# A group's closing spread over four passes, and the redo of a tied row block prepared beside the last block's products

## The chip, the cores and the metric

The kernel runs on one core of a Trainium2 chip. The metric is the device time of one execution in microseconds; times are medians of several executions. The spans, passes and waits below come from one profiled execution of each kernel.

## The reference, cut to what matters

Two graph layers work on x of 4096 rows and 256 columns. Layer 0 is an attention with four heads, masked by a 4096 x 4096 adjacency matrix; its output is normalized per row and added to x. Layer 1 makes two steps of an attention that keeps, in each row, the largest probabilities up to a sum of 0.9.

```python
e = where(adj > 0, leaky_relu(src + dst), NEG_INF)            # layer 0, four heads
out = softmax(e) @ h                                           # per head
x = x + layernorm(out) * gamma + beta                          # "closing" in the kernel
...
for n in range(2):                                             # layer 1
    A = top_p(softmax(Xa W.. ), 0.9)                           # ties: in order of index
    Xf = R @ Xf ; Xa = A @ Xa
    Z = Z + Xf @ U1[n].T + Xa @ U2[n].T
x = x + layernorm(h + Z)
```

Rows in which values tie exactly at the threshold must keep them in order of index. The kernel computes all 32 row blocks as if there were no ties, and repeats a block where there are some ("redo"). With these inputs one block of step 1 is repeated and none of step 0.

## The kernel before

Layer 0 goes over four groups of 8 row blocks. Each group has four passes (heads), each pass 16 steps `p`: VectorE makes two masks, TensorE does 32 products. What a pass leaves is evacuated in the next; after the fourth head the group is closed, in twelve small pieces ("closers": four of statistics, eight row blocks).

```python
ax = l0a.tile([P, 4, G0 * P], BF16, name="ax")                 # adjacency tile, 1 MB, by GpSimd's queue
nc.gpsimd.dma_start(ax, adj_t[...])
...
def close(i):
    xb = l0s.tile([P, D], F32, name="xb")                      # pool l0s: two buffers
    nc.sync.dma_start(xb, x[ts(b, P), :])
    ob = l0s.tile([P, D], F32, name="ob")
    nc.scalar.activation(ob, o[:, i, :], AF.Identity, scale=..., bias=...)
    nc.vector.tensor_mul(ob, ob, gamma_r)
    nc.gpsimd.tensor_tensor(xb, xb, beta_r, ALU.add)
    nc.vector.tensor_add(xb, xb, ob)
    nc.sync.dma_start(x1_d[b], xb)
    ...
# in mask_stage (SyncE and GpSimd issue the transfers)
    if h == 1 and p % 2:
        nc.sync.dma_start(adj_d[...], ax[p // 2])              # 1 MB: a copy for later
    if h == H - 1 and ig + 1 < NB // G0 and p % 2:
        next_ax.append(edges(ig + 1, p // 2))                  # next group's tiles: fourth pass
# main loop, one closer per step
    if p != PAIRS - 1 and p > 1 and later:
        later.pop(0)()                                         # three evacuations, then twelve closers
```

At the end, step 1 chooses the kept values of block 31, multiplies, contributes, and then `repaired` counts the ties and calls `again` for each tied block: logits, exponentials, a branch around a repeated search, the ranking of ties on VectorE (`untied`), and then products and contribution.

## Time and profile before

| | before |
|---|---|
| time | 3289.59 us (3287.62 to 3290.06, 3 runs) |
| span of the profiled execution | 3283.7 us |
| TensorE, VectorE, ScalarE, GpSimd busy | 90%, 81%, 59%, 38% |
| layer 0, first to last product | 801.8 us |
| the same rows as the prediction's four passes: sum | 205.1 us |

No engine is idle for long in sum, so what counts is where TensorE stops. The prediction shows the two places. The other view that matters, as it turned out, is this one: what SyncE waited for before it could issue its transfers, in the first pass after a group (337.3 to 399.8 us), where six of the eight row blocks were closed. The columns are the wait, its sum in us, how often, and the longest. In all lines PE is TensorE (PEld its weight loads), DVE VectorE, ACT ScalarE, POOL GpSimd; SPq, ACTq and POOLq are the instruction queues of SyncE, ScalarE and GpSimd.

```profile
SPq L341 <- DMA x_d<-xb: 12.1, 6, 3.5
```

Line 341 loads x rows into `xb`; before it can, the store out of the same buffer must have landed. Six such waits of at most 3.5 us did little harm: VectorE stood 0.6 us in all for the rows in that pass. The transfers' medians in that pass (KB each, us from issue to landing) were short:

```profile
x_d<-xb SPq DMA_DIRECT2D x6, 128.0 KB, 2.3
xb<-in_x_dram SPq DMA_DIRECT2D x6, 128.0 KB, 2.0
```

The share of 0.63 in the prediction's row of this pass is an average: up to 368.0 us it is 0.99, and from 374.7 us on, when the row blocks were closed, 0.36.

### The profile page before, as it was taken

The numbers are of one execution on the slowest core, as the hardware profiler recorded it, in microseconds if no ns is written. First come the engines' busy times: TensorE is split into PE (matmuls) and PEld (weight loads), VectorE is DVE, ScalarE is ACT, GpSimd is POOL, SyncE is SP. The second block draws the span as 40 slices with busy tenths as digits, with TensorE's granted clock in tenths as the row PEclk, the third lists the DMA queues.
The fourth block names the chain that finished last, engine by engine and source line by source line (L and its number), as shares of the span: only waits on it lengthen the run. The fifth ranks groups of instructions, "written<-read, shape, count | busy, mean of one in ns | idle before, by whom it ended". The sixth has DMA issues, their size and how long they took to land. (4 is left out here: it accounts for less than half of the span.)

```text
span 3283.7 us, 51700 instructions
## 1 busy us (share of the span) xinstructions
PE 2967.7 (90%) x19213; PEld 2416.0 (74%) x19213; DVE 2651.4 (81%) x5002; ACT 1950.6 (59%) x2903; POOL 1253.2 (38%) x1793
## 2 busy tenths in 40 slices
PE   4499899898989999986899999999879999999994
PEld 2399799797977888873677777777747777777783
DVE  6599899898976555555999999999479988888864
ACT  5588687786862110027577777674376777776721
POOL 3200100101000000004889889887044656656520
PEclk8699999999999999997899999999979999999997
DMA  9726639366225455420000000000200000000000
GB/s 258 229 83 154 193 115 255 115 156 191 73 93 182 163 178 164 164 76 1 13 15 17 18 15 19 17 15 20 68 2 15 25 20 25 22 22 25 20 20 12
DMA packets 198307, 268.41 MB, mean 82 GB/s; under 512 B 13728, under 2 KB 155552, under 8 KB 198048
## 3 DMA queue, kind: packets, MB, share of 16 engines
q1 hardware_dynamic: 152272, 207.99, 19.0%
q0 software_dynamic: 16896, 33.56, 5.7%
q10 hardware_dynamic: 28880, 23.48, 2.3%
q8 instruction: 153, 2.51, 0.3%
q14 instruction: 106, 0.87, 0.1%
HBM read 226.77 MB, written 71.76 MB: 91 GB/s over the span
## 5 line engine op out<-in xcount | busy, mean ns | idle before, releaser
L800 PE MATMUL acc<-X,eT 128*128 128x256 f32 x4160 | 976.2, 380 | 0.6 <-ACT eT L794 0.5
L800 PEld LDWEIGHTS acc<-X,eT 128*128 128x128 f32 x4160 | 761.8, 191 | 89.5 <-ACT eT L794 1.6
L291 PE MATMUL acc<-ut,m 128*128 128x195 bf16 (+1 forms) x8192 | 732.2, 249 | 84.0 <-DVE m L279 47.4
L291 PEld LDWEIGHTS <-m 128*128 128x128 bf16 x8192 | 704.9, 98 | 111.1 <-DVE m L279 64.8
L272 ACT ACTIVATE g<-sr,d_big 128x1024 bf16<-128x1024 f32 x512 | 550.8, 1178 | 50.7 <-DVE m L278 41.0
L618 ACT ACTIVATE void<-e,c 128x2048 int8<-128x2048 f32 x244 | 490.5, 2010 | 0.6
L432 PE MATMUL racc<-hl,ar 128*128 128x512 f32 x2048 | 470.0, 391 | 16.2 <-issue 11.1
L611 ACT ACTIVATE e<-mm,nm 128x1024 f32<-128x1024 f32 x256 | 286.2, 1118 | 332.4 <-PE mm L488 329.2
L432 PEld LDWEIGHTS racc<-hl,ar 128*128 128x128 f32 x2048 | 385.7, 189 | 100.2 <-issue 11.9
L792 PEld LDWEIGHTS tp<-ident,e 128*128 128x128 f32 x2080 | 246.5, 142 | 229.5 <-issue 142.5
L794 ACT COPY eT<-tp 128x512 f32<-128x512 f32 x520 | 304.0, 585 | 182.0 <-PE tp L792 182.0
L792 PE MATMUL tp<-ident,e 128*128 128x128 f32 x2080 | 326.6, 281 | 64.8 <-DVE e L728 35.3
L278 DVE TENSOR_TENSOR m<-g,ax 128x2048 bf16<-128x2048 bf16 x256 | 311.8, 1218 | 43.4 <-ACT g L272 39.6
L707 DVE MAX8 cand<-big 128x8 f32<-128x228 f32 (+1 forms) x1088 | 343.9, 394 | 0.1
L279 DVE TENSOR_TENSOR m<-ax,m 128x2048 bf16<-128x2048 bf16 x256 | 316.6, 1237 | 26.9 <-DVE m L278 1.4
L488 PE MATMUL mm<-kT,qT 64*128 64x512 f32 x1024 | 304.5, 678 | 33.6 <-ACT e L611 33.6
L428 DVE CAST ar<-at 128x1024 fp32r<-128x1024 bf16 x256 | 177.6, 694 | 174.0 <-PE racc L432 170.3
L694 DVE SCALAR_TENSOR_TENSOR big<-e,lowered 128x4096 f32<-128x4096 f32 x64 | 286.8, 4481 | 20.9 <-POOL lowered L639 20.9
L728 DVE SCALAR_TENSOR_TENSOR e<-e,found 128x4096 f32<-128x4096 f32 x64 | 288.2, 4503 | 0.0
L443 ACT ACTIVATE xf<-xf,rinv 128x256 f32<-128x256 f32 x64 | 32.7, 510 | 373.3 <-DVE xf L442 371.0
L648 POOL TENSOR_TENSOR sums<-sums 128x4 f32<-128x4 f32 (+1 forms) x64 | 106.3, 1661 | 353.4 <-ACT void L618 231.3
L488 PEld LDWEIGHTS mm<-kT,qT 64*128 64x128 f32 x1024 | 84.0, 195 | 130.3 <-issue 66.8
(241 smaller groups left out, 3245.8 us busy)
## 6 DMA issues: line engine op xcount, KB each, us to landing
at<-adj_d SPq DMA_DIRECT2D x256, 256.0 KB, 2.8
ut<-uv_d SPq DMA_DIRECT2D x60, 784.0 KB, 4.3
ax<-in_adj_t_dram POOLq DMA_DIRECT2D x32, 1024.0 KB, 13.1
adj_d<-ax SPq DMA_DIRECT2D x32, 1024.0 KB, 11.7
uv_d<-parts ACTq DMA_DIRECT2D x32, 392.0 KB, 7.4
xf<-xf_d SPq DMA_DIRECT2D x65, 128.0 KB, 2.0
sr<-s_d SPq DMA_DIRECT2D x16, 512.0 KB, 4.7
xf_d<-xf ACTq DMA_DIRECT2D x64, 128.0 KB, 2.2
```

The lines of the kernel that those rows point to most:

```text
L272: nc.scalar.activation(g[:, c, :], shared[k].sr, AF.Relu, scale=BIG, bias=d_big[:, h, j:j + 1])
L278: nc.vector.tensor_tensor(m[0], g, a, ALU.min)
L279: nc.vector.tensor_tensor(m[1], a, m[0], ALU.subtract)
L291: nc.tensor.matmul(shared[k].acc[i][:, t, :cols], m[t][:, c, ts(i, P)], shared[k].ut[j // QUARTER][:, j % QUARTER, t, :cols], start=(j == ...
L432: nc.tensor.matmul(acc[i].rearrange("p s d -> p (s d)"), ar[:, c, ts(i, P)], hl[hop][:, j].rearrange("p s d -> p (s d)"), start=(j == 0), ...
L488: nc.tensor.matmul(pm[:, h, :], q[ts(h, DA), :], kT[ts(h, DA), ts(c, 512)], start=True, stop=True)
L618: nc.scalar.activation(void, r.e[:, ts(h, N // 2)], (AF.Relu, AF.Sign)[i], bias=r.c1, scale=-1.0, accum_out=r.sums[:, h, 2 + i:3 + i])
L707: nc.vector.max(cand[:, s, :], big[:, edges[s]:edges[s + 1]])
L728: nc.vector.scalar_tensor_tensor(r.e, r.e, r.t, r.e, ALU.is_ge, ALU.mult, accum_out=kept)
L792: nc.tensor.transpose(pt[:, i, :], r.e[:, ts(4 * g + i, P)], ident)
L794: nc.scalar.copy(eT, pt)
L800: nc.tensor.matmul(r.acc[:, 0, :], eT[:, i, :], cur[:, j, :], start=(j == 0), stop=(j == NB - 1))
```

## The change

The intent is twofold. In layer 0 the closers are no longer done one per step in the first pass (and the start of the second), but one every third step over all four passes, so that VectorE's small surplus over TensorE can pay for them. At the end, the counting of ties and the preparation of the redo up to the ranking move in front of the products of block 31, so that VectorE ranks while TensorE multiplies.

```diff
             later = []
+            closers = []
...
-                return [both, three, divided] + (closing(ig) if h == H - 1 else [])
+                if h == H - 1:
+                    closers.extend(closing(ig))
+                return [both, three, divided]
...
-                    if p != PAIRS - 1 and p > 1 and later:
-                        later.pop(0)()
+                    if p != PAIRS - 1 and p > 1:
+                        if later:
+                            later.pop(0)()
+                        elif closers and p % 3 == 0:
+                            closers.pop(0)()
...
-    def again(n, b, kT, qT, nm, t, cur, failed):            # all of the redo, after the last block
+    def prepared(R):      # copies of q, logits, exponentials, [If failed: search], ranking
+    def completed(R, cur):  # loads, transposes, products, contribution
...
+            def beginning():
+                finish(blocks[NB - 2])
+                with tc.If(number(R, R.undone) > 0):
+                    prepared(R)
...
-                attend(r, cur, blocks.get(b - 1), blocks.get(b + AHEAD))
+                attend(blocks[b], cur, blocks.get(b - 1), blocks.get(b + AHEAD),
+                       {5: last_chosen, 6: looked} if b == NB - 2 else {})
...
+            attend(r, cur, blocks[NB - 2], None, {0: beginning})
```

(The pools `l0u` and `o` change their number of buffers too.)

More of the change, by code (lines that the diff above doesn't have):

```diff
@@ L152, in gat_then_top_p_diffusion @@
     with tc.tile_pool(name="l0", bufs=1) as l0, tc.tile_pool(name="l0a", bufs=9) as l0a, \
-            tc.tile_pool(name="l0u", bufs=6) as l0u:
+            tc.tile_pool(name="l0u", bufs=5) as l0u:
         sd_c = l0.tile([P, 2, H, NB], F32, name="sd_c")
@@ L251, in gat_then_top_p_diffusion @@
             out_rows = {}
-            later = []
+            later, closers = [], []
             def sources(k):
@@ L298, in evacuate @@
                 if h == 0:
-                    out_rows[ig] = l0o.tile([P, G0, D], F32, name="o")
+                    out_rows[ig] = l0o.tile([P, G0, D], F32, name="o", bufs=2)
                     for i in range(G0):
@@ L395, in gat_then_top_p_diffusion @@
                     products(k, p, ms.pop(n))
-                    if p != PAIRS - 1 and p > 1 and later:
-                        later.pop(0)()
+                    if p != PAIRS - 1 and p > 1:
[3 more added lines that the diff above has]
+                            closers.pop(0)()
                 later.extend(evacuate(k))
-                while later:
-                    later.pop(0)()
+                for last in later + closers:
+                    last()
     xp = ctx.enter_context(tc.tile_pool(name="xp", bufs=1))
@@ L578, in col, with totals @@
         return small.tile([P, 1], F32, name=name, bufs=bufs or 4)
-    def totals(t):
+    def totals(t, name):
         pn = ps2.tile([P, 4, P], F32, name="tp")[:, 0, :]
         nc.tensor.matmul(pn[:1, :NB], ones[:, :1], t, start=True, stop=True)
-        n = small.tile([1, 1], F32, name="n", bufs=1)
+        n = small.tile([1, 1], F32, name=f"n_{name}", bufs=1)
         nc.vector.reduce_sum(n, pn[:1, :NB], axis=AX.X)
-        n_i = small.tile([1, 1], I32, name="n_i", bufs=1)
+        n_i = small.tile([1, 1], I32, name=f"n_i_{name}", bufs=1)
         nc.vector.tensor_copy(n_i, n)
-        ns_i = small.tile([1, NB], I32, name="ns_i", bufs=1)
+        ns_i = small.tile([1, NB], I32, name=f"ns_i_{name}", bufs=1)
         nc.vector.tensor_copy(ns_i, pn[:1, :NB])
@@ L773, in untied @@
         nc.vector.scalar_tensor_tensor(r.e, ties, r.t, r.e, ALU.mult, ALU.add, accum_out=kept)
-        r.scale = col("scale")
         nc.vector.reciprocal(r.scale, kept)
@@ L820, in contributed, with attend @@
             nc.tensor.matmul(r.acc[:, 1, :], zT[:, i, :], u_s[2 * r.n + i // KC][:, i % KC, :], start=(i == 0), stop=(i == 3))
-    def attend(r, cur, before, ahead):
+    def attend(r, cur, before, ahead, between={}):
         if ahead:
@@ L844, in attend, with questioned @@
                 first_probe(ahead, PROBED.index(g))
+            if g in between:
+                between[g]()
         scaled(r)
-    def again(n, b, kT, qT, nm, t, cur, failed):
-        sp, dve, act = b
-        r = SimpleNamespace(n=n, b=sp)
-        q = rows.tile([2 * DA, P], F32, name="a_q", bufs=1)
-        shift = col("a_nm", 1)
-        nc.scalar.copy(q, qT[:, ds(act * P, P)])
-        nc.scalar.copy(shift, nm[:, ds(act, 1)])
-        r.e = l1e.tile([P, N + NB], F32, name="e1")[:, :N]
-        sums = small.tile([P, 2, 4], F32, name="sums", bufs=6)
-        ev = r.e.rearrange("p (h c n) -> p h c n", h=2, c=4)
-        loads(r)
-        z, r.t = col("a_z", 1), col("a_t", 1)
-        def exponentials_again():
-            for c in range(4):
-                nc.scalar.activation(ev[:, :, c, :], logits(q, kT, c), AF.Exp, bias=shift, accum_out=sums[:, c // 2, c % 2:c % 2 + 1])
-            nc.vector.tensor_tensor(sums[:, 0, :2], sums[:, 0, :2], sums[:, 1, :2], ALU.add)
-            nc.vector.tensor_tensor(z, sums[:, 0, 0:1], sums[:, 0, 1:2], ALU.add)
-        exponentials_again()
-        nc.vector.tensor_copy(r.t, t[:, ds(dve, 1)])
-        if n + 1 < STEPS:
-            r.x = rows.tile([P, D], F32, name="a_x", bufs=1)
-            nc.vector.tensor_copy(r.x, X[:, ds(dve, 1), :].rearrange("p o d -> p (o d)"))
-        with tc.If(failed > 0):
-            m = small.tile([P, N // 1024], F32, name="m4", bufs=1)
-            for c in range(N // 1024):
-                nc.vector.tensor_reduce(m[:, c:c + 1], logits(q, kT, c), AX.XY, ALU.max)
-            nc.vector.tensor_reduce(shift, m, AX.X, ALU.max, negate=True)
-            exponentials_again()
-            searched(r.e, z, r.t, junk)
-        untied(r, z, junk)
-        eT = [turn(r, 0)]
-        for g in range(NB // 4):
-            if g + 1 < NB // 4:
-                eT.append(turn(r, g + 1))
-            gather(r, eT[g], g, cur)
-        scaled(r)
-        contributed(r, contribute(r))
-        finish(r)
-        finish_scale(r)
-        finish_rows(r)
-    def repaired(n, kT, qT, nm, far, cur, found):
+    everyone = [ET.PE, ET.DVE, ET.Activation, ET.Pool, ET.SP]
+    def questioned(far, found):
         t, after, eighth = found
@@ L906, in repaired @@
         nc.vector.tensor_tensor(undone, undone, failed, ALU.add)
-        engines = dict(engines=[ET.PE, ET.DVE, ET.Activation, ET.Pool, ET.SP], min_val=0, max_val=6 * P * NB)
-        with tc.If(nc.values_load(totals(undone)[1], **engines) > 0):
-            numbers = totals(failed)[1]
-            failed_n = nc.values_load(numbers, **engines)
-            counts = totals(undone)[0]
-            which, key, ids = (small.tile([1, NB], F32, name=f"a_{x}", bufs=1) for x in ("which", "key", "ids"))
-            nc.vector.tensor_scalar(which, counts, 0, None, ALU.is_gt)
-            blocks_n = small.tile([1, 1], F32, name="a_n", bufs=1)
-            blocks_i = small.tile([1, 1], I32, name="a_ni", bufs=1)
-            nc.vector.reduce_sum(blocks_n, which, axis=AX.X)
-            nc.vector.tensor_copy(blocks_i, blocks_n)
-            nc.vector.tensor_tensor_scan(key, ones[:1, :NB], zero[:1].to_broadcast([1, NB]), 0.0, ALU.add, ALU.add)
-            nc.vector.tensor_tensor(key, key, which, ALU.mult)
-            for i in range(NB // 8):
-                nc.vector.max(ids[:, ts(i, 8)], key)
-                nc.vector.match_replace(key, ids[:, ts(i, 8)], key, -1.0)
-            ids_i, rest = (small.tile([1, NB], I32, name=f"a_{x}", bufs=1) for x in ("ids_i", "rest"))
-            nc.vector.tensor_scalar(ids_i, ids, -1.0, 0.0, ALU.add, ALU.max)
-            with tc.For_i(0, nc.values_load(blocks_i, engines=engines["engines"], min_val=0, max_val=NB), 1):
-                b = [nc.values_load(ids_i[:, :1], engines=[x], min_val=0, max_val=NB - 1) for x in (ET.SP, ET.DVE, ET.Activation)]
-                again(n, b, kT, qT, nm, t, cur, failed_n)
-                nc.vector.tensor_copy(rest[:, 1:], ids_i[:, 1:])
-                nc.vector.tensor_copy(ids_i[:, :NB - 1], rest[:, 1:])
@@ new lines, in questioned, with counted, number @@
+        return failed, undone
+    def counted(R):
+        R.undone, R.failed = totals(R.undone, "u"), totals(R.failed, "f")
+        R.e = l1e.tile([P, N + NB], F32, name="e1")[:, :N]
+        R.z, R.t, R.scale = (col(f"a_{x}", 1) for x in ("z", "t", "scale"))
+        R.rest_i = small.tile([1, 1], I32, name="a_rest_i", bufs=1)
+        R.ids_i = small.tile([1, NB], I32, name="a_ids_i", bufs=1)
+    def number(R, total):
+        return nc.values_load(total[1], engines=everyone, min_val=0, max_val=6 * P * NB)
@@ new lines, in chosen @@
+    def chosen(R):
+        which, key, ids = (small.tile([1, NB], F32, name=f"a_{x}", bufs=1) for x in ("which", "key", "ids"))
+        nc.vector.tensor_scalar(which, R.undone[0], 0, None, ALU.is_gt)
+        blocks_n = small.tile([1, 1], F32, name="a_n", bufs=1)
+        nc.vector.tensor_tensor_scan(key, ones[:1, :NB], zero[:1].to_broadcast([1, NB]), 0.0, ALU.add, ALU.add)
+        nc.vector.tensor_tensor(key, key, which, ALU.mult)
+        for i in range(NB // 8):
+            nc.vector.max(ids[:, ts(i, 8)], key)
+            nc.vector.match_replace(key, ids[:, ts(i, 8)], key, -1.0)
+        nc.vector.tensor_scalar(R.ids_i, ids, -1.0, 0.0, ALU.add, ALU.max)
+        nc.vector.reduce_sum(blocks_n, which, axis=AX.X)
+        nc.vector.tensor_scalar(R.rest_i, blocks_n, -1.0, None, ALU.add)
@@ new lines, in index, with exponentials_again @@
+    def index(R, engine):
+        return nc.values_load(R.ids_i[:, :1], engines=[engine], min_val=0, max_val=NB - 1)
+    def prepared(R):
+        act, dve = index(R, ET.Activation), index(R, ET.DVE)
+        q = rows.tile([2 * DA, P], F32, name="a_q", bufs=1)
+        shift = col("a_nm", 1)
+        nc.scalar.copy(q, R.qT[:, ds(act * P, P)])
+        nc.scalar.copy(shift, R.nm[:, ds(act, 1)])
+        nc.vector.tensor_copy(R.t, R.table[:, ds(dve, 1)])
+        sums = small.tile([P, 2, 4], F32, name="sums", bufs=6)
+        ev = R.e.rearrange("p (h c n) -> p h c n", h=2, c=4)
+        def exponentials_again():
+            for c in range(4):
+                nc.scalar.activation(ev[:, :, c, :], logits(q, R.kT, c), AF.Exp, bias=shift, accum_out=sums[:, c // 2, c % 2:c % 2 + 1])
+            nc.vector.tensor_tensor(sums[:, 0, :2], sums[:, 0, :2], sums[:, 1, :2], ALU.add)
+            nc.vector.tensor_tensor(R.z, sums[:, 0, 0:1], sums[:, 0, 1:2], ALU.add)
+        exponentials_again()
+        with tc.If(number(R, R.failed) > 0):
+            m = small.tile([P, N // 1024], F32, name="m4", bufs=1)
+            for c in range(N // 1024):
+                nc.vector.tensor_reduce(m[:, c:c + 1], logits(q, R.kT, c), AX.XY, ALU.max)
+            nc.vector.tensor_reduce(shift, m, AX.X, ALU.max, negate=True)
+            exponentials_again()
+            searched(R.e, R.z, R.t, junk)
+        untied(R, R.z, junk)
@@ new lines, in completed @@
+    def completed(R, cur):
+        r = SimpleNamespace(n=R.n, b=index(R, ET.SP), e=R.e, scale=R.scale)
+        dve = index(R, ET.DVE)
+        loads(r)
+        if r.n + 1 < STEPS:
+            r.x = rows.tile([P, D], F32, name="a_x", bufs=1)
+            nc.vector.tensor_copy(r.x, X[:, ds(dve, 1), :].rearrange("p o d -> p (o d)"))
+        eT = [turn(r, 0)]
+        for g in range(NB // 4):
+            if g + 1 < NB // 4:
+                eT.append(turn(r, g + 1))
+            gather(r, eT[g], g, cur)
+        scaled(r)
+        contributed(r, contribute(r))
+        finish(r)
+        finish_scale(r)
+        finish_rows(r)
+        rest = small.tile([1, NB], I32, name="a_rest", bufs=1)
+        nc.vector.tensor_copy(rest[:, 1:], R.ids_i[:, 1:])
+        nc.vector.tensor_copy(R.ids_i[:, :NB - 1], rest[:, 1:])
@@ L932, in finish, with repaired @@
+    def repaired(R, cur):
+        with tc.If(number(R, R.undone) > 0):
+            completed(R, cur)
+            with tc.For_i(0, nc.values_load(R.rest_i, engines=everyone, min_val=0, max_val=NB), 1):
+                prepared(R)
+                completed(R, cur)
     def finish(r):
@@ L999, in gat_then_top_p_diffusion, with chosen_kept @@
                 probed(3)
-            for b in range(NB):
+            def chosen_kept(b):
                 r = blocks[b]
@@ L1022, in gat_then_top_p_diffusion, with last_chosen, looked @@
                     masked(r)
+            R = SimpleNamespace(n=n, kT=kT, qT=qT, nm=nm, table=found[0])
+            def last_chosen():
+                chosen_kept(NB - 1)
+                R.failed, R.undone = questioned(far, found)
+            def looked():
+                counted(R)
+                chosen(R)
+            def beginning():
+                finish(blocks[NB - 2])
+                with tc.If(number(R, R.undone) > 0):
+                    prepared(R)
+            for b in range(NB - 1):
+                chosen_kept(b)
                 if b + AHEAD < NB:
                     blocks[b + AHEAD] = began(n, b + AHEAD, kT, qT, nm, sg, thr, c1)
-                attend(r, cur, blocks.get(b - 1), blocks.get(b + AHEAD))
+                attend(blocks[b], cur, blocks.get(b - 1), blocks.get(b + AHEAD),
+                       {5: last_chosen, 6: looked} if b == NB - 2 else {})
             r = blocks[NB - 1]
-            finish(blocks[NB - 2])
+            attend(r, cur, blocks[NB - 2], None, {0: beginning})
             contributed(r, contribute(r))
@@ L1033, in gat_then_top_p_diffusion @@
                 finish_rows(blocks[b])
-        repaired(n, kT, qT, nm, far, cur, found)
+        repaired(R, cur)
 _INS = ['x', 'adj', 'adj_t', 'w', 'a', 'gamma', 'beta', 'w1_t', 'w2_t', 'w3_t', 'u1_t', 'u2_t', 'ln_g', 'ln_b']
```

## The prediction

> **What bounds the kernel now.** I read the page first (busy shares and slices), then the chain of waits that ended last, then the timeline of two places that the change touches, and last the busy time of single stretches. The page says that TensorE is busy 90% of 3283.7 us, VectorE 81%, so no engine has enough idle time for a large win; a gain has to come from places where TensorE waits. Two such places are changed.
>
> The first is the end. The chain that ended last, in order of time (start us, us, what; cut in the middle and at the end):
>
> ```profile
> 3226.52 2.35 DVE junk L758
> ...
> 3233.40 4.33 DVE rank L768
> ...
> 3240.41 4.50 DVE rank L768
> ...
> 3247.32 4.50 DVE e L773 x2
> 3251.82 0.14 issue
> 3251.96 1.94 PE tp L792 x8
> 3253.90 3.54 PE acc L800 x8
> ```
>
> This is the redo of the one row block with tied values in step 1 (64 blocks should give 4096 product matmuls counted as on the page, it shows 4160: one block more). The timeline of that stretch shows what TensorE does meanwhile (start, us, engine, line, operation, idle before and its releaser):
>
> ```profile
> 3203.95 0.18 DVE L585 TENSOR_REDUCE n<-tp 1x1 f32<-1x32 f32 x1 [15.66 <-PE tp L583]
> ...
> 3217.50 6.50 PE L488 MATMUL mm<-kT,a_q 64*128 64x512 f32 x16 [10.03 <-ACT a_q L853]
> ...
> 3251.96 1.94 PE L792 MATMUL tp<-ident,e 128*128 128x128 f32 x8 [27.96 <-DVE e L773]
> ```
>
> TensorE stands still for 10.03 us, works 6.5 us on logits, and stands still for another 27.96 us while VectorE ranks the ties; just before that VectorE itself was idle 15.66 us, in the last block's products. The two idle times don't overlap, and nothing but program order keeps them apart.
>
> The second place is layer 0. I cut its 16 passes (4 groups of rows by 4 heads, 512 matmuls each) at the first product of each. Busy time in the four passes of the second group (window, length, then PE, PEld, DVE, ACT, POOL, granted clock, DMA share, GB/s):
>
> ```profile
> 337.30:399.80 62.50, 48.97 (x515) 45.19 (x513) 53.76 (x85) 40.34 (x51) 10.83 (x11) 0.95 0.63 200
> 399.80:450.20 50.40, 46.39 (x512) 44.56 (x512) 46.73 (x49) 41.73 (x55) 6.61 (x6) 0.97 0.45 128
> 450.20:496.30 46.10, 44.45 (x515) 43.42 (x513) 42.19 (x38) 39.35 (x50) 0.00 (x0) 1.00 0.25 82
> 496.30:542.40 46.10, 44.44 (x515) 43.42 (x514) 41.86 (x38) 39.37 (x50) 5.18 (x7) 1.00 1.04 250
> ```
>
> The first two passes carry the closing of the group before. A pass without it takes 46.1 us (46.6 us where it evacuates the first head), so the closing costs 16.4 + 3.8 = 20.2 us, three times: 60.6 us. The closing of the fourth group comes after the last product and stays there.
>
> **What the Trainium skill says.** (1) "TensorE: Matmul & The Clock Gate", What's actually happening: the array falls to half clock after an idle window of some 3.4 us. The trace agrees: the eight transposes at 3251.96 took 1.94 us against 1.07 us for eight in mid-block, and the first eight products 3.54 us against 1.73 us a group later. (2) "SBUF — State Buffer", Who interferes with whom: a GpSimd operation and a VectorE operation in a two-port mode block each other. The trace fits: some mask subtractions take 1.57 us instead of 1.23 us in the passes where GpSimd adds beta, none in the others. (3) "Runtime: NRT & Kernel Launch", Instruction fetch mechanics: a taken branch to a far target stalls the fetch. The trace agrees: at the end of step 0, where nothing is redone, VectorE's jump over the redo took 3.1 us from its compare (2340.70) to its next instruction (2343.83), TensorE's 1.05 us.
>
> **Part 1, layer 0.** The same 12 closers are kept per group, one after every third step at p = 6, 9, 12 of four passes (p = 3 goes to the evacuation), as the order of instructions confirms. From the timeline: a mask pair on VectorE comes every 2.46 us, TensorE takes 2.72 us per step, so VectorE gains 0.26 us a step. The evacuation's three adds use up the lead until p = 6. A pair of statistics costs VectorE 1.08 us (356.13 to 357.21), a closed row block 1.53 us (377.78 to 379.32). With zero lead at p = 6, the lead regained before a closer bites is 0.5 us for the first and 0.75 us for the second and third, 2.0 us per pass; the rest is stall.
> - Pass of three statistics: 3 x 1.08 - 2.0 = 1.2 us.
> - One statistics, two closes: 1.08 + 3.06 - 2.0 = 2.1 us. This pass also starts with VectorE's row sums of the first head, which ScalarE's evacuation awaits. VectorE now comes there 1.7 us later than after a free pass (evacuation 2.0 us before the pass turns; now about 0.3). I add 1.7 us; today's pass, late in the same way, begins with a step of 4.74 instead of 3.54 us.
> - Two passes of three closes: 2 x (4.6 - 2.0) = 5.2 us.
> - Eight additions on GpSimd that now mostly hit a mask operation: 6 x 0.34 = 2 us.
>
> Together 12.2 us per group against 20.2: 8 us x 3 = 24 us. Today's dear items, two steps of 7.0 and 6.4 us where the first closed block waits for GpSimd's power (2.68 us) and then ScalarE, vanish, because 8 us pass between last statistics and first close; I take 26 us. The buffer for weights going from 6 to 5 costs nothing: a quarter is loaded two ahead and at most four are live.
>
> **Part 2, the end.** Now the last block's choice is made in the products of block 30, the counts there too (two small matmul groups, 0.3 us on TensorE), and logits, exponentials and tie ranking of the redo come after the first group of products of block 31. Working forward from the old times: group 0 of block 31 ended at 3188.7, +0.3 is 3189.0; indices are on hand at about 3185.2 (counts 3181.4, 1.2 us of reads, 2.6 us of choosing as from 3213.87 to 3216.39) and ScalarE's copy of q at about 3188.6, so the logits start at 3189.3. TensorE is warm there: instead of 7.9 us (3217.50 to 3225.40) to the last exponential I estimate 6.2, ScalarE's four at 1.1 us each with the logits between them. Sums 0.5 us and the skipped search 0.8 us: ranking starts at 3196.8 and takes its 25.4 us, to 3222.2. TensorE meanwhile resumes block 31 at about 3196 with 14.9 us of products and 3.9 us of contribution, done near 3215, 7 us before: VectorE still sets the time. The redo's transposes start at 3222.2 instead of 3251.96: **29.8 us** earlier, and the 31.7 us from there to the end are unchanged, the cold start too, since 7 us idle is enough.
>
> Step 0 redoes nothing and pays: counts 0.3 us and one more branch on TensorE (load 0.5, compare 0.4, fetch 1.05 us, of which matmuls queued ahead hide about 1.5): +0.8 us. VectorE's second jump lies in its own idle time there.
>
> **Sum.** -26 - 29.8 + 0.8 = -55 us: 3289.6 - 55 = **3234.6 us**, 1.7% less.
>
> **The rivals.** (a) Spreading hides the closing nearly wholly: only the 8 us of VectorE work above its slack would go, for example if ScalarE's wait at the pass start (2.33 us VectorE idle) absorbed more; 3 x 17 us saved, then 3210 us. For it: VectorE is idle some 4 us in a free pass; against it: most of that idle time lies at the pass start, before the closers. (b) Spreading moves the stalls to four passes and saves little, because every closer meets an empty lead, and in-order GpSimd or SyncE queues hold the adjacency loads back: 8 us or less saved, 3252 us. For it: the lead is 0 at p = 6. Against it: the long waits of today (7.0 and 6.4 us) have a named cause that goes away. (c) Branch costs: ranking begins late because all five engines must load the count and fetch the body; or TensorE stalls in block 31 until ranking ends, so that 19 us of products follow it. Then part 2 saves about 11 us: 3253 us. Against it: the built order has the transposes of block 31 wait only on TensorE and ScalarE.
>
> **Range and chances.** Part 1 I hold to -16 to -36, part 2 to -25 to -32 net. Added as independent errors this gives about 10 us each way: 3225 to 3245. Faster by over 2% needs 65.8 us, which is rival (a): 0.12. Slower by over 2% would need a new wait of 120 us: 0.01. Within 2%: 0.87.
>
> **What would show it.** Passes with closers should last 47.3, about 50.4, 48.7 and 48.7 us plus up to 1 us for GpSimd, in place of 62.5, 50.4, 46.1, 46.1; no step over 4 us but the first of the second pass. The ranking's first operation should start about 8 us after the redo's logits and TensorE's wait for it shrink from 28 to about 7 us, after block 31's contribution. In step 0 the last block should be 1 us longer. The prediction is wrong if the third and fourth pass are still 46.1 us (rival a), if GpSimd or SyncE waits appear before the masks (b), or if block 31's products follow the ranking (c).

## More of the kernel before

PE, VectorE, ScalarE and GpSimd run in the order of the program here; SyncE's transfers are ordered by the scheduler.

## The result, and the profile after

| | before | after |
|---|---|---|
| time, same rounds | 3288.61 us (3284.26 to 3290.06, 4 runs) | 3262.58 us (3259.72 to 3262.82, 4 runs) |
| ratio | | 0.9921, 95% interval 0.9904 to 0.9938: the same at 2% |
| span of the profiled execution | 3283.7 us | 3260.9 us |
| layer 0, first to last product | 801.8 us | 804.4 us |
| redo's first transposes after block 31's first product in step 1 | 65.0 us | 37.2 us |

Ratios here and below are the mean time of one kernel's fast runs over that of the other's of the same rounds, so not quite the ratio of the medians quoted beside them. The change gained 26 us where 55 were predicted, outside the range. The end gained nearly its part (65.0 - 37.2 = 27.8 us); layer 0, predicted at -26 us, got 2.6 us longer.

**Layer 0.** The same four passes as in the prediction, by their busy times (window, length, then PE, PEld, DVE, ACT, POOL, granted clock, DMA share, GB/s):

```profile
336.80:384.50 47.70, 45.10 (x515) 43.25 (x513) 43.23 (x56) 37.93 (x45) 0.00 (x0) 1.00 0.70 226
384.50:436.00 51.50, 46.03 (x512) 43.16 (x512) 47.41 (x52) 41.12 (x56) 10.92 (x8) 1.00 0.26 84
436.00:485.10 49.10, 44.99 (x515) 43.21 (x514) 46.62 (x50) 40.70 (x53) 2.38 (x2) 1.00 0.48 135
485.10:546.60 61.50, 47.20 (x515) 44.64 (x513) 48.74 (x51) 40.79 (x53) 13.44 (x14) 0.92 1.05 274
```

The first three passes came out as predicted (47.3, 50.4, 48.7 and about 1 more). The fourth took 61.5 us instead of 48.7, and it is the one whose DMA share is above 1. The third set of closers, in the fourth group, is the control: no next group's adjacency is loaded there, and its passes lasted 47.7, 51.2, 49.5 and 49.0 us, 197.4 in all against 205.4 before. So that group saved 8.1 us, as predicted, while the second and third lost 4.8 and 6.0 us against the kernel before.

Within the fourth pass one step, p = 13, took 12.04 us and the next 5.64 us; a step of TensorE's own is 2.72 us. The 12.04 us hold the wait that follows; the 5.64 us are its echo, for the granted clock averages 0.57 from 538.2 to 543.9 us (hence the 0.92 in the pass's row). The timeline around it (start, us, engine, line, operation, idle before and its releaser; other rows left out):

```profile
504.36 10.63 SPq L381 DMA_DIRECT2D adj_d<-ax  x2
...
507.76 0.98 DVE L348 TENSOR_TENSOR xb<-xb,ob 128x256 f32<-128x256 f32 x1
...
515.09 0.46 SPq L349 DMA_DIRECT2D x_d<-xb  x1
...
529.29 0.33 SPq L343 DMA_DIRECT2D xb<-in_x_dram  x1
...
535.20 0.72 POOL L347 TENSOR_TENSOR xb<-xb,beta_r 128x256 f32<-128x256 f32 x1 [13.40 <-DMA xb<-in_x_dram]
535.96 0.42 DVE L348 TENSOR_TENSOR xb<-xb,ob 128x256 f32<-128x256 f32 x1 [9.93 <-POOL xb L347]
```

Read it from the bottom. VectorE stood 9.93 us for GpSimd, GpSimd for the load of x rows, and SyncE issued that load only at 529.29. It waited for the store at 515.09 out of the same buffer, and this store was itself issued 6.4 us after VectorE had finished the row block (508.74). What SyncE did meanwhile stands in its own waits in that pass:

```profile
SPq L381 <- DMA ax<-in_adj_t_dram: 27.2, 3, 10.2
SPq L343 <- DMA x_d<-xb: 21.9, 3, 13.2
```

Line 381 is the copy of the adjacency tiles. The scheduler has pulled it forward from the second pass of the next group to right behind each tile's load, so SyncE waits there for a 1 MB load to land, and the small store stands behind it. In the kernel before it did the same (39.8 us of such waits in that pass), but no row of x was moved there. When the store is issued, the 1 MB write of 514.62 is ahead of it on the same queue; in the trace's transfer records that queue moves the write's packets (told by their size) until about 526 us, and the store's from 526.0 to 528.8 us. Then the load needs 6 us. From VectorE's addition to GpSimd's next use of the buffer this is 535.20 - 508.74 = 26.5 us. A buffer comes up again after two closers, six steps or some 16.3 us; the difference is 10 us, which is VectorE's wait. The medians of the whole stretch from 485 to 550 us:

```profile
ax<-in_adj_t_dram POOLq DMA_DIRECT2D x7, 1024.0 KB, 13.7
adj_d<-ax SPq DMA_DIRECT2D x6, 1024.0 KB, 11.8
x_d<-xb SPq DMA_DIRECT2D x3, 128.0 KB, 9.9
xb<-in_x_dram SPq DMA_DIRECT2D x3, 128.0 KB, 6.8
```

The stores took 9.9 us instead of 2.3, the loads 6.8 instead of 2.0. The Trainium skill, "DMA: Bandwidth & Descriptors", Queues, rings and completion order, says that each DMA engine takes the descriptors of a ring in their order. The 128 KB store that moves ten microseconds after it was issued, behind a 1 MB write, agrees.

**The end.** TensorE's last waits (the same view as in the prediction):

```profile
3193.00 1.99 PE L493 MATMUL mm<-kT,a_q 64*128 64x512 f32 x8
...
3228.36 1.94 PE L796 MATMUL tp<-ident,e 128*128 128x128 f32 x8 [11.51 <-DVE e L778]
```

The wait of 10.03 us for the count has gone and that of 27.96 us is 11.51. The order is the intended one: logits at 3193.00 inside block 31, ranking beside its products. One wait is longer than predicted, the one before the ranking's first operation, before the change and after it:

```profile
3226.52 2.35 DVE L758 TENSOR_SCALAR junk<-e,a_t 128x4096 uint8<-128x4096 f32 x1 [0.74 <-DVEq L872]
```
```profile
3202.65 2.35 DVE L763 TENSOR_SCALAR junk<-e,a_t 128x4096 uint8<-128x4096 f32 x1 [3.26 <-DVEq L919]
```

The releaser is VectorE's own sequencer at the inner branch, which skips the repeated search: the same code as before, 2.5 us more.

### The profile page after: what moved, and what is told of

It reads as the page before. It is cut to its first block, busy times and chain, and to the rows that moved or that the text cites. A ratio compares the mean times of both kernels' runs of the same rounds, so it can differ in the third digit from the quotient of the medians.

```text
span 3260.9 us, 51761 instructions
## 1 busy us (share of the span) xinstructions
PE 2966.0 (91%) x19213; PEld 2411.7 (74%) x19213; DVE 2657.5 (81%) x5020; ACT 1948.7 (60%) x2903; POOL 1132.7 (35%) x1793
## 5 line engine op out<-in xcount | busy, mean ns | idle before, releaser
L291 PEld LDWEIGHTS <-m 128*128 128x128 bf16 x8192 | 697.6, 97 | 120.7 <-DVE m L279 67.3
L796 PE MATMUL tp<-ident,e 128*128 128x128 f32 x2080 | 326.7, 281 | 47.7 <-DVE e L733 33.6
L448 ACT ACTIVATE xf<-xf,rinv 128x256 f32<-128x256 f32 x64 | 32.6, 510 | 374.5 <-DVE xf L447 372.4
```

The costliest lines, as they stand in the source:

```text
L291: nc.tensor.matmul(shared[k].acc[i][:, t, :cols], m[t][:, c, ts(i, P)], shared[k].ut[j // QUARTER][:, j % QUARTER, t, :cols], start=(j == ...
L796: nc.tensor.transpose(pt[:, i, :], r.e[:, ts(4 * g + i, P)], ident)
```

## The experiments

Theory A: the rows of x are caught between two buffers, SyncE's order and the adjacency transfers of the fourth pass, and this ate layer 0's gain. Theory B: the spreading does pay, and the end failed. Theory C: the fourth pass's transfers are too much by themselves. Experiments 1 to 4 and 5 to 8 ran with the kernel before in the same rounds at 3304.39 us and 3302.14 us, some 15 us slower than in the first measurement. Each call ran on another chip, so only ratios are compared across.

**1. Layer 0's part alone**, on the kernel before:

```diff
 (kernel before)
+ closers of layer 0 spread as in the change; l0u 5 buffers, o 2 buffers
```

> Only the layer-0 part of the change, on the kernel before (the end untouched). Theory A (the 12 us wait in the fourth passes of groups 1 and 2 eats what the spreading saves): the sums of the four passes are 205.1 before and 209.8, 211.1, 197.4 after, so the 16 passes together should be about 3 us longer than before, and the run 3288.6 + 3 = about 3291.5 us, the same within 0.3%. Rival B (the spreading works as predicted and the end part is what failed): about 3263 us.

Measured: 3307.16 us (3306.41 to 3310.03), ratio 1.0005 (0.9985 to 1.0025). Its profile has the fourth passes at 61.6 and 61.5 us. The part gains nothing alone.

**2. The end's part alone**:

```diff
 (changed kernel)
- closers of layer 0 spread
+ layer 0 of the kernel before
```

> Only the end part (the redo prepared beside the last block), layer 0 as before. Theory A: the redo's transposes 27 us earlier, 0.8 us lost at the very end and 1 us in step 0: 3288.6 - 25 = about 3263.5 us, faster by 0.8%, passes of 62.5, 50.4, 46.1 and 46.1 us again. Rival B: about 3288 us.

Measured: 3279.91 us (3274.02 to 3281.72), ratio 0.9918 (0.9896 to 0.994). All of the change's gain is the end's. Theory B falls.

**3. Eight buffers for the rows of x**, nothing else:

```diff
-                    xb = l0s.tile([P, D], F32, name="xb")
+                    xb = l0s.tile([P, D], F32, name="xb", bufs=8)
```

> The changed kernel with eight buffers in place of two for the rows of x that a closed row block reads, so that the load of a row block waits for no store of the same group. Theory A (the load of the eighth row block waits for the store two row blocks before, which lies behind the adjacency transfers of the fourth pass): the step of 12.0 to 12.5 us falls to about 3.5 us, the fourth pass to about 49 us as in the last group, twice; 3262.6 - 25 = about 3238 us, the predicted size of part 1. Rival C (the transfers of the fourth pass are simply too much, or GpSimd's queue stands behind its own adjacency loads): the step of 12 us stays and the time is 3262 us within 3.

Measured: 3262.18 us (3260.61 to 3265.27), ratio 0.9869 (0.9849 to 0.9889). The fourth pass of the second group, and its transfers:

```profile
489.50:540.00 50.50, 45.48 (x515) 43.22 (x514) 47.63 (x50) 40.84 (x53) 13.47 (x14) 1.00 1.05 249
```
```profile
x_d<-xb SPq DMA_DIRECT2D x3, 128.0 KB, 15.7
xb<-in_x_dram SPq DMA_DIRECT2D x1, 128.0 KB, 13.5
```

Layer 0 became 22.3 us shorter than in the change, where 25 were expected. This run settles most of it. The DMA share is 1.05 as before and the rows' transfers are even slower, 15.7 and 13.5 us, and yet the pass lasts 50.5 instead of 61.5 us: a slow transfer harms only where a buffer waits for it. Theory C, in the form that the transfers' amount costs the time, falls.

**4. No closers in the fourth pass**, four in each of the other three:

```diff
-                        elif closers and p % 3 == 0:
+                        elif closers and k % H != H - 1 and p in (6, 9, 12, 14):
```

> The changed kernel with the same closers at p = 6, 9, 12 and 14 of the first three passes, none in the fourth. Theory A: fourth pass 46.1 us, the first about 48.3, the second about 53, the third about 51: sum 198.4 in place of 210 to 211, twice 12 us and nothing in the last group: about 3238 us. Rival C (the adjacency transfers are slow in themselves): also no 12 us step in the fourth pass here if the closers are its victims only, but if the store of the third pass still waits, the steps move to the first pass of the next group and the time stays near 3262 us.

Measured: 3257.91 us (3255.85 to 3261.64), ratio 0.9852 (0.9833 to 0.9872). The fourth pass lasts 46.9 us, with the adjacency transfers still filling it (share 1.01):

```profile
493.90:540.80 46.90, 44.25 (x515) 43.34 (x513) 45.06 (x40) 39.36 (x50) 10.57 (x11) 1.00 1.01 236
```

Two remedies that share nothing but the wait of the rows of x both give most of the missing 28.6 us: layer 0 is 22.3 and 23.6 us shorter than in the change.

**5. The copies of the adjacency by GpSimd's queue**, whose order is the program's, so that they come after all the loads:

```diff
-                        nc.sync.dma_start(adj_d[ts(p // 2, 4), ...
+                        nc.gpsimd.dma_start(adj_d[ts(p // 2, 4), ...
```

> The changed kernel, but the eight 1 MB writes of each group's adjacency tiles go through GpSimd's queue, in the second pass of the group where the program has them, instead of SyncE's queue, whose order had pulled them forward to the fourth pass of the group before, each right behind the load that it waits for. Theory A (the rows of x stand behind these writes on SyncE: the wait for the load, then the transfer): the step of 12 us in the fourth pass of groups 1 and 2 goes back to under 4 us, the fourth passes last about 50.5 us as with eight buffers, ratio to the kernel before 0.986 to 0.989 like experiment 3. Theory C (the loads of the adjacency alone fill the DMA engines and delay any row of x): the long step stays, at 8 us or more, ratio about 0.992. Rival: the writes now collide in the second pass, which then grows by several us and eats the gain.

Measured: 3261.05 us (3259.11 to 3262.49), ratio 0.9873 (0.9857 to 0.989). The fourth passes are 50.3 and 50.5 us, no step over 4.1 us, with two buffers:

```profile
493.40:543.80 50.40, 45.34 (x516) 43.31 (x514) 47.56 (x50) 40.87 (x53) 15.46 (x16) 1.00 0.98 213
```
```profile
x_d<-xb SPq DMA_DIRECT2D x3, 128.0 KB, 6.9
xb<-in_x_dram SPq DMA_DIRECT2D x2, 128.0 KB, 5.5
```

Not all copies went to the second pass: four were issued from 542.8 to 545.1 us, right after the last load, and four in the second pass. The loads of the next adjacency still keep the DMA engines full (0.98), but with the copies off SyncE both round trips of this pass, from the issue of a store to the landing of the load into the same buffer, take 14.3 us (517.12 to 531.42 and 526.02 to 540.31), which fits into the 16.3 us of two closers. So of the two kinds of large transfer it was the copies on SyncE's queue that the two buffers could not bear. The edit takes them out of SyncE's order and out of most of the fourth pass at once, so it does not say which of the two helped. The second pass did not grow (51.7 and 51.1 us).

**6. The rows of x on ScalarE's queue**, each store issued one closer later so that ScalarE need not wait:

```diff
+                    if i > 0:
+                        nc.scalar.dma_start(x1_d[b - 1], stored.pop())
                     xb = l0s.tile([P, D], F32, name="xb")
-                    nc.sync.dma_start(xb, x[ts(b, P), :])
+                    nc.scalar.dma_start(xb, x[ts(b, P), :])
...
-                    nc.sync.dma_start(x1_d[b], xb)
+                    stored.append(xb)
```

> The changed kernel, still with two buffers for the rows of x, but their loads and stores are issued by ScalarE, which has no other transfers in layer 0: the store of a row block is issued one closer later, so ScalarE never waits for VectorE's addition. The 1 MB loads and writes stay where they are. If the order on SyncE's queue is the cause (theory A), a store lands in 3 to 5 us although the DMA engines are as full as before, the 12 us steps go to under 4 us, ratio 0.986 to 0.990. If the DMA engines' load itself is the cause (theory C), stores still take 10 us and more, and the long step stays (fourth pass 58 us or more, ratio about 0.992). ScalarE's two more issues per closer should cost it well under 1 us each, which it has free.

Measured: 3271.19 us (3260.12 to 3276.12), ratio 0.9907 (0.9891 to 0.9924). It lands between the theories. The fourth passes are 56.7 and 58.3 us, the long step 6.5 us instead of 12, with 5.5 us after it.

```profile
x_d<-xb ACTq DMA_DIRECT2D x4, 128.0 KB, 7.4
xb<-in_x_dram ACTq DMA_DIRECT2D x3, 128.0 KB, 9.1
```

Away from SyncE's order the rows still take 7.4 and 9.1 us beside 16 full DMA engines. The edit also holds back the loads: ScalarE issues a load in its own order, right after the store that waits for VectorE's addition, and no longer when its buffer comes free. The last load was issued at 521.48 us, though the store out of its buffer had landed at 517.43; that is 4.1 us, about VectorE's whole wait of 4.41 us for this row block. So the edit does not tell how much was SyncE's order and how much the engines' load. The Trainium skill, "DMA: Bandwidth & Descriptors", Issuing engines are not separate DMA queues, says that transfers of all issuers share the 16 engines and that a second issuer saves only issuing time; the slow landings agree with the first half.

**7. Experiments 3 and 4 together**, `bufs=8` and no closer in the fourth pass.

> Experiments 3 and 4 together: eight buffers for the rows of x, and four closers in each of the first three passes, none in the fourth. Under theory A the buffers have nothing left to give when the closers stay out of the fourth pass: ratio 0.985 as in experiment 4, within 0.002. If the buffers also remove smaller waits in the first three passes (51.2 and 51.0 us in experiment 4), these get up to 2 us shorter each, and the ratio falls to about 0.983.

Measured: 3249.88 us (3236.01 to 3255.19), ratio 0.9843 (0.9826 to 0.986), 0.0009 under experiment 4, inside its interval. The second and third passes went from 51.2 and 51.0 to 52.2 and 49.4 us, so the buffers move little more.

**8. Without the repeated search** in the inner branch, which these inputs never take (the result was right):

```diff
             exponentials_again()
-            searched(R.e, R.z, R.t, junk)
         untied(R, R.z, junk)
```

> The changed kernel without the repeated search inside the inner branch of the prepared redo (it is never run on these inputs, so the result stays right). Theory: the 3.26 us that VectorE stands before the ranking is its jump over that search, which took 0.74 us in the kernel before. Then the wait before the ranking's first operation falls to 0.5 to 1.0 us, the redo's transposes start about 2.5 us earlier relative to block 31, and the jumps over the redo in step 0 get no longer; time about 2.5 us (0.1%) below the changed kernel's, ratio about 0.991. Rival: the wait is for the fetch of the instructions behind any branch, whatever is skipped: then it stays at about 3 us.

Measured: 3272.04 us (3268.99 to 3274.63), ratio 0.9903 (0.9886 to 0.992); 2.5 us can't be resolved in the time. The profile resolves them: the wait before the ranking and TensorE's for the transposes are

```profile
3214.45 2.35 DVE L763 TENSOR_SCALAR junk<-e,a_t 128x4096 uint8<-128x4096 f32 x1 [0.57 <-ACT eT L798]
```
```profile
3240.16 1.94 PE L796 MATMUL tp<-ident,e 128*128 128x128 f32 x8 [8.82 <-DVE e L778]
```

0.57 instead of 3.26 us (now put down to another releaser) and 8.82 instead of 11.51: the skipped code costs 2.7 us here. The traces also show what differs from the kernel before. In the changed kernel the branch's compare ends at 3199.69, a transfer of 16 KB of instructions runs from 3201.20 to 3202.15, and VectorE's next instruction comes at 3202.47, after 2.78 us; experiments 2 and 9 look the same (2.87 and 2.77 us). In the kernel before, such a transfer ran from 3223.75 to 3224.67, ahead of the compare's end at 3225.81, and the next instruction came after 0.53 us; in experiment 8 there is none, and it came after 0.16 us. So the slow skip is the one with that transfer inside it. The records don't name the engine that a transfer is for, and no run moved the branch alone, so that VectorE waited for it is argued, and why it came late stays open.

**9 and 10. The changed kernel and experiment 7's, side by side**, five rounds (4 runs of the mended kernel and 9 of the kernel before are on record), kernel before at 3294.91 us (3288.53 to 3301.7).

> The changed kernel itself, unedited, so that it stands on the same chip and in the same rounds as the candidate of experiment 10; the earlier experiments ran on another chip than the first measurement. Expected: ratio to the kernel before 0.992 within 0.002, the fourth passes of groups 1 and 2 again near 62 us in its profile.

> The kernel of experiment 7 again, beside the changed kernel. From the profiles, layer 0 of experiment 7 was about 13 us per group 1 and 2 shorter than the changed kernel's, 27 us in all with step 0 as fast as there. Expected: ratio to the kernel before 0.984 to 0.986, so 0.7 to 0.8% under experiment 9. If experiment 7's advantage came from a lucky step 0 in its profiled run (its runs spread from 3236 to 3255 us), the difference to experiment 9 falls to 0.3%.

Measured: the changed kernel 3270.8 us (3263.36 to 3274.38), ratio 0.9925 (0.9911 to 0.9939), fourth passes 61.5 and 63.1 us; the mended one 3246.51 us (3241.88 to 3251.48), ratio 0.9853 (0.9836 to 0.9869). That is 0.9853 / 0.9925 = 0.9927, so 0.7% or 24 us under the change, and 1.5% under the kernel before: it beats both.

Layer 0 in the profiles, passes of the second group and first to last product of the layer, in us:

| kernel | pass 1 | 2 | 3 | 4 | sum | layer 0 |
|---|---|---|---|---|---|---|
| before | 62.5 | 50.4 | 46.1 | 46.1 | 205.1 | 801.8 |
| change | 47.7 | 51.5 | 49.1 | 61.5 | 209.8 | 804.4 |
| 3, eight buffers | 47.7 | 52.7 | 48.6 | 50.5 | 199.5 | 782.1 |
| 4, none in fourth | 48.8 | 51.2 | 51.0 | 46.9 | 197.9 | 780.8 |
| 5, copies moved | 47.7 | 51.7 | 49.1 | 50.3 | 198.8 | 780.4 |
| 6, own queue | 47.7 | 51.2 | 49.7 | 56.7 | 205.3 | 797.0 |
| 7, both | 48.8 | 52.2 | 49.4 | 46.9 | 197.2 | 777.6 |

## Why the prediction was right or wrong

- **Part 1, "Two passes of three closes: 2 x (4.6 - 2.0) = 5.2 us": the step that failed.** It counted VectorE's work in the fourth pass and left out that a closed row block needs its rows of x through a load and a store on SyncE, in two buffers. The third pass agreed (49.1 us for 48.7); the fourth took 61.5 us, because the buffer's round took 26.5 us where two closers leave 16.3. Part 1 came out at +2.6 us instead of -26. The prediction had the warning in its own lines: the row of the fourth pass with DMA share 1.04. It read those rows for length only, did not see that until then the row blocks were closed at a share of 0.36, and never asked what the closers would meet in a pass in which they had never run.
- **"12.2 us per group against 20.2": right where that wait is absent.** In the fourth group, with no adjacency to load, the four passes exceed free ones (46.6 + 3 x 46.1 = 184.9 us) by 197.4 - 184.9 = 12.5 us. In the second group it is 14.6 us with eight buffers. So the arithmetic of VectorE's lead was good, and with the wait mended layer 0 saves 19.7 to 24.2 us of the 26.
- **Rival (b)** named the right place, in-order queues on GpSimd or SyncE, but had the victim wrong (the adjacency loads) and the size small: it gave part 1 a saving of up to 8 us. Its sign, "if GpSimd or SyncE waits appear before the masks", is what the trace shows. "The long waits of today have a named cause that goes away" was true and no protection from a new one.
- **The buffer of weights from 6 to 5 costs nothing:** never tested alone, but the first three passes and the whole fourth group agree with the sum without it.
- **Part 2, 29.8 us: the mechanism right, one term short.** The redo's first transposes came 23.6 us earlier in the span and block 31 began 4.2 us later, so 27.8 us of 29.8. The logits (3193.0, predicted 3189.3 + 4.2) and the exponentials (6.0 us, predicted 6.2) were as expected; the term "the skipped search 0.8", which the kernel before had suggested, measured 3.26 us; the prediction's own third point, a jump of 3.1 us on VectorE, had shown that a skip can cost so much. TensorE's wait of "about 7 us" was 11.51, because the ranking began late and block 31 ended 2 us earlier than estimated; VectorE still set the time. The tail after the transposes was 32.6 us instead of 31.7.
- **Step 0, +0.8 us:** its last block lasted 16.90 instead of 16.23 us, +0.7.
- **The sum:** the miss in the profiled span, 55 - 22.8 = 32.2 us, is 28.6 us of layer 0, 2.8 us of the end (2.0 before the transposes, 0.8 after), and some 1 us of scatter between the two executions. Which of SyncE's order, place in the queue and full engines makes how much of the 26.5 us is not settled; experiment 5 shows that moving the copies suffices, and experiment 6 came out between.

## What to carry to other kernels

When work is moved into another stage, list everything that it uses, its small transfers and buffers too, and look up in that stage's row whether the queue and the DMA engines are free there; the engine's arithmetic alone is half a prediction. A round trip through a buffer (last use, store issued, store landed, load landed) must fit into the time until the buffer comes up again, and one landing time from a quiet stage says nothing about a full one. A group that differs in one condition only, like the last group here, is a control that the trace gives for free.

## What the Trainium skill lacked or had wrong

- "DMA: Bandwidth & Descriptors", Issuing engines are not separate DMA queues: it holds that issuing from another engine saves only the sequencer's issuing time. Here it also took the small transfers out of SyncE's order, whose waits for 1 MB loads reached 10.2 us; the long step fell from 12 to 6.5 us although ScalarE issued a load 4.1 us after its buffer was free. (The rows were then also on a queue without 1 MB transfers; no run separates the two.) The page gives no landing time for a small transfer beside large ones; here a 128 KB store took 2.3 us at DMA share 0.36, and 9.9 us at 1.05.
- "Runtime: NRT & Kernel Launch", Instruction fetch mechanics: it says that a branch stalls when its target has to be fetched first, without a size. From the compare to VectorE's next instruction the skip of the same body took 0.53 us in the kernel before and 2.78 us in the changed one, where a 16 KB transfer of instructions lay in between, and 0.16 us when the body was nearly empty. Why the transfer came earlier in the one kernel no run here shows.
- "SBUF — State Buffer", Who interferes with whom: it tells that GpSimd blocks where a VectorE operation holds the shared ports, but not that two such streams can settle into different phases. Blocks 1 to 30 of step 0, whose code the change leaves alone but for the end, took 724.2 us in the changed kernel's profile and 742.8 us in experiment 1's. In both, GpSimd operations of 128 elements last 4 to 5 us where they meet VectorE's long operations (4.48 us), but which lines meet them differs; in the second it is one on the way to what VectorE waits for (changed kernel first, then experiment 1; busy us, mean ns):

```profile
L643 POOL TENSOR_TENSOR lowered<-inv_e,a 128x1 f32<-128x1 f32 x26 | 16.0, 615 | 2.2
```
```profile
L643 POOL TENSOR_TENSOR lowered<-inv_e,a 128x1 f32<-128x1 f32 x27 | 118.1, 4373 | 2.3
```

  In experiment 1 VectorE waited 24 times for GpSimd there, 14.7 us in all, and in the changed kernel's profile never. Over all twelve profiles the stretch grows with this wait (between 1640 and 2300 us): 724.2 to 726.4 us in the four without it, 726.9 to 730.1 us with 1.8 to 3.1 us of it, 737.4 to 743.4 us with 9.2 to 14.7 us. The kernel of experiment 7 alone spread from 3236 to 3255 us. That the phase is the cause of such scatter is argued from these rows, not shown by an experiment. Its 19 us are as much as layer 0's part of several ratios above, and so the profile's stretches, not the times, carry those readings.
